# Moving one 1.7 MB load two places down the SyncE queue in the opening of a sparse GATv2 + GCN kernel

## The chip, the cores and the metric

One Trainium2 chip, one core. The metric is the device time of the whole program in microseconds, as a median of runs. A profiled execution is a separate execution of the same program, with its own time.

## What is computed

The input is a feature matrix `x` (3327 x 128, padded to 3328 rows, 26 blocks of 128) and a dense-stored adjacency `adj` (3328 x 3328, float32, about 2% of it nonzero). Two graph layers run one after the other, each on a layer-normed and rectified copy of `x`, and each is added back to `x`:

```
# layer 0: four GATv2 heads
E   = leaky_relu(h @ w1 [:,None,:] + h @ w2 [None,:,:])   # every pair i,j
s   = exp(8 * tanh((E @ a) / 8)) * adj                    # zero where adj is zero
s   = s / sum(s, -1)
out = leaky_relu(s @ h @ Wlin.T)      # heads concatenated, then @ w
# layer 1: GCN
relu(D^-1/2 (adj + I) D^-1/2 @ (h @ W.T + b))
```

Because `adj` zeroes most pairs, the kernel only forms the pairs of each row's nonzero columns. It lists them per row, and gathers the features of those columns.

## The kernel before

**Tables.** In DRAM there are two tables of 3329 rows x 720 floats. One row belongs to one graph node j. Columns 64 and up hold j's features, its part of the score and its products `h_j @ w2` for four heads; columns 0 to 63 hold the adjacency weights of j towards 64 rows of the block in work, so table 0 serves the lower half of a block (`hb` = 0) and table 1 the upper half (`hb` = 1). Columns 64 and up are built once, in the opening, as seven "images" in SBUF (`img`, lines 1022 to 1064, four blocks of 128 nodes each, the last one two blocks) and are stored to both tables by `store(i, t)` (L1041 to L1043; 1312 KB each, 656 KB for the last). Columns 0 to 63 are written anew for each half block by `weights(b, hb)` (L568 to L573), a DRAM to DRAM copy of 832 KB from the transposed adjacency `AT_d`.

**One block.** `load(b)` (L340 to L342) brings the 128 adjacency rows of block b into `adjb`, a pool of one buffer, so a load must wait until the block before it is done with the buffer; the last reader is the row sum at L426. `prep(b)` (L344 to L545) then codes the nonzeros on VectorE (L401), picks them with max instructions (L405 and after), transposes the rows on TensorE (L355), copies them out on ScalarE (L357) and stores them to `AT_d` from ScalarE's queue (L360). The pairs of a half block are processed in nine groups: `gather` (L551 to L566) issues indirect gathers from GpSimd (L562), one for each of eight slots of a buffer `g`; each such window of eight serves two groups, four windows and a smaller one (`ge`, three gathers) make a half block. `stage_z` (L576) transposes a group's rows on TensorE into `z` (L587) and applies the relu as a maximum on VectorE (`r`, L599); `stage_r` (L604) multiplies by `a` (L610); `finish` (L614) does the softmax weights and the weighted sum.

**Order.** Everything is under a hand-written schedule. The main loop (L1146 to L1159) walks over the groups, and `slot()` (L812) between them advances the preparation of the next block by a fixed amount and issues gathers. So each engine's instruction order is fixed when the program is built, and an engine that waits for one instruction holds up all that stands behind it. SyncE (SP) issues `x`, `adj`, the image stores, `weights` and the `hTb` loads, all in one DMA queue (q1 on the page); ScalarE's DMAs are q10, GpSimd's gathers q0.

**The opening.** L1104 to L1135 compute the seven images, store each to table 0 as soon as it is done (L1064), prepare block 0 in between, and then store all seven to table 1 (L1128, L1129). In this last loop, `load(1)` stands behind one of the stores. After it come `weights(0, 1)`, the end of block 0's preparation and the main loop.

**Buffers that overlap.** The four gather buffers (`pg0` to `pg3`, L1138, 23,040 bytes in each partition) are opened when the images' pools (10,496 bytes each, L963) are closed, and lie in the same SBUF. By the addresses of the built program, `pg0` covers the small constants and image 0; `pg1` covers the last 544 bytes of image 0, images 1 and 2 and the first part of image 3; `pg2` covers the rest of image 3, image 4 and the first part of image 5; `pg3` the rest of image 5 and image 6. A gather into `pg1` therefore waits until images 0 to 3 have been stored to table 1, one into `pg2` until images 4 and 5 have, one into `pg3` until image 6 has.

Of the kernel before, what the change touches and what calls it, by code (L numbers as in the profile page):

```python
# [228 lines left out]
def _sparse_layers(tc, nc, x, adj, w1, w2, a, wlin, w, gw, gb, gb_sb, gwT, x_sb, dinv, flag, ident, out):  # L229
# [15 lines left out]
    NB = NP // P  # L245
# [8 lines left out]
    with ExitStack() as l0:  # L254
# [85 lines left out]
        def load(b):  # L340
            blks[b].adjb = pa.tile([P, NP], F32, name="adjb")
            nc.sync.dma_start(blks[b].adjb, adj[b * P:(b + 1) * P, :])  # L342
# [225 lines left out]
        def weights(b, hb):  # L568

            assert blks[b].turned  # L570
            c0 = b % 4 * P + HALF * hb
            nc.sync.dma_start(tables[hb][:NP, :HALF].rearrange("(p r) c -> p r c", p=P),
                              AT_d[b // 4 * NP:(b // 4 + 1) * NP, c0:c0 + HALF].rearrange("(p r) c -> p r c", p=P))  # L573
# [197 lines left out]
        def advance(upto):  # L771

            for b in range(NB):
                while done[b] < NPREP and b * NPREP + done[b] < upto:
                    if next(preps[b], "end") == "end":
                        done[b] = NPREP
                    else:
                        done[b] += 1
                        assert done[b] < NPREP
# [171 lines left out]
        with tc.tile_pool(name="pre", bufs=1) as pre, ExitStack() as images:  # L951
# [36 lines left out]
            def norm(b0, n):  # L988

                st6 = pre.tile([P, n, 6], F32, name=f"st{b0}")  # L990
                for k in range(n):
                    nc.vector.bn_stats(st6[:, k], x_sb[:, b0 + k])
                    nc.vector.bn_aggr(mean[:, b0 + k], st6[:, k])
                var = pre.tile([P, n], F32, name=f"var{b0}")
                nc.vector.tensor_scalar(var, mean[:, b0:b0 + n, 1], EPS, None, op0=OP.add)
                neg = pre.tile([P, n], F32, name=f"neg{b0}")
                nc.vector.tensor_scalar(neg, mean[:, b0:b0 + n, 0], -1.0, None, op0=OP.mult)
                rstd = pre.tile([P, n], F32, name=f"rstd{b0}")
                for _ in inv_root(rstd, var):
                    pass  # L1000
                cen = cens[b0]
                for k in range(n):
                    if b0:
                        nc.gpsimd.tensor_scalar(cen[:, k], x_sb[:, b0 + k], neg[:, k:k + 1], 0.0, op0=OP.add, op1=OP.max)
                    else:
                        nc.scalar.activation(cen[:, k], x_sb[:, b0 + k], AF.Relu, bias=neg[:, k:k + 1], scale=1.0)
                return cen, rstd

            def weights_of_scores():


                nc.vector.tensor_mul(prod, w2_sb, a_bc)
                nc.vector.tensor_reduce(wa[:, :H], prod, AX.X, OP.add)
                nc.vector.tensor_mul(prod, w1_sb, a_bc)
                nc.vector.tensor_reduce(wa[:, H:2 * H], prod, AX.X, OP.add)
                nc.vector.tensor_scalar(wa[:, 2 * H:], wa[:, H:2 * H], SLOPE, None, op0=OP.mult)
                nc.vector.tensor_scalar(wa[:, :H], wa[:, :H], SLOPE, None, op0=OP.mult)

            K = -(-NB // 4)
            imgs, hTs = {}, {}  # L1020

            def features(i):

                b0, n = 4 * i, min(4, NB - 4 * i)
                img = room[i]
                nc.gpsimd.memset(img[:, :n, P + H:PROJ - FEAT], 1.0)
                nc.gpsimd.memset(img[:, :, COLS - FEAT:], 0.0)
                cen, rstd = normed.pop(b0)
                nc.vector.tensor_mul(img[:, :n, :P], cen, rstd[:, :, None].to_broadcast([P, n, D]))
                imgs[i] = img  # L1030

            def turn(i):
                b0, n = 4 * i, min(4, NB - 4 * i)
                pt = ps_s.tile([P, BANK], F32, name="s")
                for k in range(n):
                    nc.tensor.transpose(pt[:, k * P:(k + 1) * P], imgs[i][:, k, :P], ident)
                hTs[i] = turned[i % 2]
                nc.scalar.copy(hTs[i][:, :n * P], pt[:, :n * P])
                nc.scalar.dma_start(hT_d[:, b0 * P:(b0 + n) * P], hTs[i][:, :n * P])

            def store(i, t):  # L1041
                b0, n = 4 * i, min(4, NB - 4 * i)
                nc.sync.dma_start(tables[t][b0 * P:(b0 + n) * P, FEAT:].rearrange("(b p) c -> p b c", p=P), imgs[i][:, :n, :])  # L1043

            def products(i):

                b0, n = 4 * i, min(4, NB - 4 * i)
                img, hT = imgs[i], hTs.pop(i)
                pzs = []
                for k0 in range(0, n, 2):  # L1050
                    pz = ps_z.tile([P, 2, BANK], F32, name="z")
                    for k in range(min(2, n - k0)):
                        nc.tensor.matmul(pz[:, k, :], hT[:, (k0 + k) * P:(k0 + k + 1) * P], w2_sb.rearrange("p h d -> p (h d)"),
                                         start=True, stop=True)
                    pzs.append(pz)
                px = ps_a.tile([P, 2, 256], F32, name="ag")[:, 0, :12 * H].rearrange("p (k c) -> p k c", k=4)
                for k in range(n):
                    nc.tensor.matmul(px[:, k, :], hT[:, k * P:(k + 1) * P], wa, start=True, stop=True)
                for k0, pz in zip(range(0, n, 2), pzs):
                    m = min(2, n - k0)  # L1060
                    nc.scalar.copy(img[:, k0:k0 + m, PROJ - FEAT:COLS - FEAT], pz[:, :m, :])
                nc.scalar.copy(img[:, :n, P:P + H], px[:, :n, :H])
                nc.scalar.copy(p_all[:, b0:b0 + n, :], px[:, :n, H:])
                store(i, 0)  # L1064
# [25 lines left out]
            with tc.manual_schedule():  # L1090
                normed = {}

                def norms():
                    lo, hi = spans.pop(0)
                    cen, rstd = norm(lo, hi - lo)
                    for b0 in range(lo, hi, 4):
                        part = slice(b0 - lo, min(b0 + 4, hi) - lo)
                        normed[b0] = cen[:, part], rstd[:, part]

                def ahead(n):  # L1100
                    while len(made) < min(n, K):
                        made.append(features(len(made)))

                made = []  # L1104
                norms()
                ahead(1)
                advance(2)
                weights(0, 0)
                turn(0)
                blks[0].hTb = pb.tile([P, P], F32, name="hTb")  # L1110
                nc.sync.dma_start(blks[0].hTb, hT_d[:, :P])
                weights_of_scores()
                if len(spans):
                    norms()
                ahead(3)
                products(0)
                if K > 1:
                    turn(1)
                if len(spans):
                    norms()  # L1120
                ahead(5)
                for i in range(1, K):
                    if i + 1 < K:
                        turn(i + 1)
                    products(i)
                    advance(2 + NCODE * i / (K - 1))
                    ahead(i + 3)
                for i in range(K):  # L1128
                    store(i, 1)  # L1129
                    if i == min(1, K - 1) and NB > 1:  # L1130
                        load(1)
                weights(0, 1)
                advance(NLIST)
                turn_parameters()
                advance(NPREP)  # L1135
# [93 lines left out]
def kernel(  # L1229
# [26 lines left out]
    gb_sb = const.tile([P, D], F32, name="gb_sb")  # L1256

    _sparse_layers(tc, nc, x, adj, w1, w2, a, wlin, w, gw, gb, gb_sb, gwT, x_sb, dinv, flag, ident, out)


# [46 lines left out]
```

## Time and profile before

| | us |
|---|---|
| median of three runs | 3246.03 (3227.53, 3246.03, 3260.07) |
| profiled execution, its own time | 2536.74 |
| span of the profiled execution | 2534.9 |
| TensorE busy | 2278.9 (90%) |
| VectorE busy | 2030.5 (80%) |
| GpSimd busy | 1791.8 (71%) |
| mean granted TensorE clock | 0.980 |

DMA moved 838.58 MB at a mean of 331 GB/s, and its busy share is 9 tenths or more in all but the last of the 40 slices. The span is counted from the first to the last instruction of the program; the profiled execution is 709 us shorter than the median of the runs, and the page does not say where the runs spend these 709 us.

How to read the views: in the timeline a row is "start, duration, engine, line, operation, out<-in, count", and what stands in square brackets is how long the engine sat idle before it and what ended that. An entry of SPq is the issuing of a DMA, not its data. In the queue view a row gives a DMA queue's packets, its MB and the time that they took as a share of 16 DMA engines in that stretch. In the view by stretches a row gives each engine's busy time and, at the end, the granted TensorE clock, the DMA busy share and GB/s.

### The profile page before, as it was taken

Reading aid. Unit: us, or ns where it says so; the run is one execution under the profiler, and the core shown is the slowest. Engines: PE = TensorE matmul, PEld = TensorE weight load, DVE = VectorE, ACT = ScalarE, POOL = GpSimd, SP = SyncE. Lnnn points to the kernel's source line nnn. Section 1 sums busy time; section 2 is a strip of 40 time slices with the busy share of each in tenths; the row PEclk is TensorE's granted clock in tenths of the full one; section 3 lists DMA queues with packets and bytes.
Section 4 is the critical chain, followed back from the end, with each engine's and each line's share of the span. In section 5 each row is a group of like instructions: output and inputs, shape, how many; then the busy total and the mean of one; then the engine's idle time right before and its main releaser. Section 6 shows DMA issues by size and latency. Waiting matters only on the chain.

```text
span 2534.9 us, 51974 instructions
## 1 busy us (share of the span) xinstructions
PE 2278.9 (90%) x19410; PEld 1586.2 (63%) x19410; DVE 2030.5 (80%) x6260; ACT 704.1 (28%) x1651; POOL 1791.8 (71%) x1873
## 2 busy tenths in 40 slices
PE   6689899988989998989998999999999899999898
PEld 4456666656666666666666666666666667675553
DVE  7678988888788888878888788988988888895433
ACT  4122233223223222322322322232232233222110
POOL 3577777777777777777777777777777777777620
PEclk9789999999999999999999999999999999999999
DMA  9999999999999999999999999999999999999995
GB/s 294 392 338 314 342 353 318 334 351 335 324 339 346 318 328 359 329 319 343 337 312 336 353 311 341 352 329 329 339 346 318 330 360 313 333 322 347 324 336 186
DMA packets 460759, 838.58 MB, mean 331 GB/s; under 512 B 209099, under 2 KB 318165, under 8 KB 457173
## 3 DMA queue, kind: packets, MB, share of 16 engines
q0 software_dynamic: 145600, 640.34, 71.0%
q1 hardware_dynamic: 219396, 140.96, 19.1%
q10 hardware_dynamic: 95504, 53.88, 7.0%
q8 instruction: 156, 2.56, 0.4%
q14 instruction: 103, 0.84, 0.1%
HBM read 765.93 MB, written 113.42 MB: 347 GB/s over the span
## 4 chain that ended last, share of the span: by engine, by line
PE 35%; DVE 24%; DMA 20%; POOL 11%; issue 7%; ACT 1%; SPq 0%; DVEq 0%; POOLq 0%; ACTq 0%
DMA g<-table,idx 13%; DVE r L599 11%; POOL g L562 10%; PE z L587 10%; PE s L610 6%; PE z L590 3%; DMA ge<-table,idxo 3%; PE z L937 2%; DVE cand L405 2%; PE tr L627 2%; PE ag L658 2%; DMA AT_d<-at 2%; PE tr L370 2%; PE tr L505 1%; DVE codes L401 1%
## 5 line engine op out<-in xcount | busy, mean ns | idle before, releaser
L562 POOL DMA_INDIRECT g<-table,idx x1664 | 1616.3, 971 | 568.3 <-issue 442.2
L599 DVE TENSOR_TENSOR r<-z,x1n 128x1024 f32<-128x1024 f32 x832 | 1010.1, 1215 | 65.5 <-PE z L587 63.9
L587 PE MATMUL z<-ident,g 128*128 128x128 f32 x6656 | 922.4, 278 | 151.9 <-DVE r L599 111.7
L587 PEld LDWEIGHTS z<-ident,g 128*128 128x128 f32 x6656 | 743.8, 142 | 366.9 <-DVE r L599 224.2
L610 PE MATMUL s<-r,sel 128*32 128x512 f32 (+1 forms) x3744 | 491.1, 597 | 0.7 <-ACT ssb L618 0.7
L618 ACT COPY ssb<-s 128x512 f32<-128x512 f32 x260 | 146.7, 564 | 524.6 <-PE s L610 522.5
L630 DVE TENSOR_TENSOR sc<-tr,g 128x32 f32<-128x32 f32 x208 | 38.5, 185 | 300.5 <-PE tr L627 300.5
L405 DVE MAX8 cand<-codes 128x8 f32<-128x52 uint16 x1664 | 215.3, 205 | 0.0
L562 POOL DMA_INDIRECT ge<-table,idxo x156 | 152.6, 978 | 47.5 <-issue 38.1
L638 ACT ACTIVATE th<-sc 128x32 f32<-128x32 f32 x260 | 58.3, 224 | 420.9 <-DVE sc L633 418.5
L590 PE MATMUL z<-oi,x1b 128*128 128x384 f32 x416 | 174.1, 501 | 0.0
L658 PEld LDWEIGHTS ag<-g,wt 128*32 128x32 f32 x3328 | 99.0, 110 | 115.3 <-issue 100.8
L357 ACT COPY at<-tr 128x512 f32<-128x512 f32 (+1 forms) x175 | 97.0, 554 | 222.2 <-PE tr L355 198.3
L627 PE MATMUL tr<-ident,ssb 128*128 128x128 f32 x988 | 153.1, 276 | 5.0 <-ACT ssb L618 4.5
L610 PEld LDWEIGHTS s<-r,sel 128*32 128x32 f32 x3744 | 73.9, 108 | 110.5 <-issue 86.4
L587 PEld LDWEIGHTS z<-ident,ge 128*128 128x128 f32 x624 | 81.4, 146 | 94.8 <-issue 28.5
L596 ACT ACTIVATE r<-z 128x768 f32<-128x768 f32 x104 | 84.3, 810 | 201.7 <-PE z L590 201.7
L658 PE MATMUL ag<-g,wt 128*32 128x133 f32 x3328 | 133.4, 278 | 0.0
L587 PE MATMUL z<-ident,ge 128*128 128x128 f32 x624 | 111.7, 283 | 21.1 <-DMA ge<-table,idxo 18.5
L627 PEld LDWEIGHTS tr<-ident,ssb 128*128 128x128 f32 x988 | 114.3, 141 | 15.3 <-ACT ssb L618 14.9
L355 PE MATMUL tr<-ident,adjb 128*128 128x128 f32 x676 | 107.4, 282 | 16.3 <-DMA adjb<-in_adj_dram 10.2
L401 DVE SCALAR_TENSOR_TENSOR codes<-adjb,code 128x832 uint16<-128x832 f32 x104 | 102.3, 1020 | 1.9 <-DMA adjb<-in_adj_dram 1.9
(188 smaller groups left out, 2350.4 us busy)
## 6 DMA issues: line engine op xcount, KB each, us to landing
adjb<-in_adj_dram SPq DMA_DIRECT2D x26, 1664.0 KB
table<-AT_d SPq DMA_DIRECT2D x52, 832.0 KB
AT_d<-at ACTq DMA_DIRECT2D x150, 256.0 KB
g<-table,idx POOLq DMA_INDIRECT x1664
table<-img SPq DMA_DIRECT2D x12, 1312.0 KB
adjb<-AT_d SPq DMA_DIRECT2D x18, 512.0 KB
g<-AT_d SPq DMA_DIRECT2D x7, 1024.0 KB
g<-AT_d ACTq DMA_DIRECT2D x5, 1024.0 KB
```

Of the source, the lines that this page charges most:

```text
L355: nc.tensor.transpose(pt[:, q, :], adjb[:, (j0 + q) * P:(j0 + q + 1) * P], ident)
L357: nc.scalar.copy(at[:, :n, :], pt[:, :n, :])
L401: nc.vector.scalar_tensor_tensor(codes[:, i], adjb[:, c0:c0 + part], 0.0, code[:, c0:c0 + part], op0=OP.not_equal, op1=OP.mult, accum_out= ...
L405: nc.vector.max(cand[:, c, 8:].rearrange("p (r s) -> p r s", s=32)[:, :, sgm % 32], codes.rearrange("p a b -> p (a b)")[:, sgm % 32 * SEG: ...
L562: return nc.gpsimd.indirect_dma_start(out=g[:, t, lo:COLS], out_offset=None, in_=tab, in_offset=bass.IndirectOffsetOnAxis(ap=at[:, t:t + 1 ...
L587: nc.tensor.matmul(z[:, i, q * P:(q + 1) * P], g[:, m % 2 * 4 + q, PROJ + h * D:PROJ + (h + 1) * D], ident, is_transpose=True, start=(q == ...
L590: nc.tensor.matmul(z[:, i, :n], k.x1b[:, h * D:(h + 1) * D], k.oi[:, hb * n:(hb + 1) * n], start=False, stop=True, skip_group_check=True)
L599: nc.vector.tensor_tensor(r.rearrange("p h (i s) -> p h i s", s=16), z.rearrange("p h (i s) -> p h i s", s=16), k.x1n[:, 2 * hp:2 * hp + 2 ...
L610: nc.tensor.matmul(k.s[32 * h:32 * h + 32, :n], sel[:, h, 31 - at:63 - at], rs[h // 2][:, h % 2, :n], start=(at == 0), stop=(at == 1 or m ...
L618: nc.scalar.copy(ssb[:, :nk * P], s[:, :nk * P])
L627: nc.tensor.transpose(pt[:, q, :], ssb[:, q * P:(q + 1) * P], ident)
L658: nc.tensor.matmul(ag[32 * cg:32 * cg + 32, u, :WORK], wt[:, t].rearrange("p h q -> p (h q)"), g[:, t, FEAT:FEAT + WORK], start=(w == 0 an ...
```

## The change

```diff
@@ -1127,7 +1127,7 @@
                     ahead(i + 3)
                 for i in range(K):
                     store(i, 1)
-                    if i == min(1, K - 1) and NB > 1:
+                    if i == min(3, K - 1) and NB > 1:
                         load(1)
                 weights(0, 1)
                 advance(NLIST)
```

K is 7. In the built program no engine but SP has another order. On SP's queue the load of block 1's adjacency rows (1664 KB), which stood between the table 1 stores of images 1 and 2, now stands between those of images 3 and 4:

```
 L1043 DMACopy table_74<-img_160 128x4x656
 L1043 DMACopy table_74<-img_164 128x4x656
-L342 DMACopy adjb<-in_adj_dram 128x3328
 L1043 DMACopy table_74<-img_168 128x4x656
 L1043 DMACopy table_74<-img_172 128x4x656
+L342 DMACopy adjb<-in_adj_dram 128x3328
 L1043 DMACopy table_74<-img_176 128x4x656
 L1043 DMACopy table_74<-img_180 128x4x656
```

No instruction is added or removed. Which stores a gather waits for stays the same; only the semaphores that carry these waits are dealt out anew.

## The prediction

> **What bounds the kernel now.** I read the page first, then the view by stretches, then the chain of waits in order of time, the timelines of SP, GpSimd, VectorE and TensorE from 55 to 140 us, and the queue view by stretches. The stretches show two regimes (columns: span; busy time and count of PE, PEld, DVE, ACT, POOL; clock; DMA share; GB/s):
>
> ```profile
> 90.00:99.00 9.00, 0.00 (x0) 0.00 (x0) 2.74 (x10) 0.58 (x1) 6.72 (x7) 0.70 1.06 396
> 99.00:133.00 34.00, 27.12 (x210) 18.00 (x211) 25.99 (x84) 7.49 (x14) 25.23 (x27) 0.88 1.05 397
> 190.00:1200.00 1010.00, 913.96 (x8168) 644.10 (x8168) 856.47 (x2633) 293.99 (x698) 762.86 (x785) 0.99 0.99 335
> ```
>
> From 190 us on TensorE is busy 90% of the time and DMA runs at 335 GB/s. In the opening DMA moves 396 GB/s and TensorE stands still for 9 us. So the steady part is bound by compute, and the change can act only in the opening, where the bytes are the bound. The chain of waits agrees: its longest piece is the table 1 stores.
>
> ```profile
> 61.27 0.87 SPq L342
> 62.18 1.24 SPq L1043
> 63.47 26.13 DMA table<-img
> 89.75 0.70 issue
> 90.45 4.21 DMA g<-table,idx
> 94.97 7.64 DMA g<-table,idx
> 102.65 2.18 PE z L587 x9
> ```
>
> GpSimd issues the first window (w0) at 67.13 to 77.6 us, and then waits for image 3's store before the second (w1); TensorE waits for w1's rows:
>
> ```profile
> 90.45 1.71 POOL L562 DMA_INDIRECT g<-table,idx  x1 [12.88 <-DMA table<-img]
> ...
> 99.19 0.45 PE L587 MATMUL z<-ident,g 128*128 128x128 f32 x1 [9.97 <-DMA table<-img]
> ```
>
> The second row starts 99.19 - 90.45 = 8.7 us after the gather was issued; its release is put down to a store, but what it reads is the gather. On VectorE, block 1's coding of the adjacency stands in front of the first relu:
>
> ```profile
> 73.63 0.22 DVE L536 TENSOR_TENSOR pmx<-tmask,p_all 128x64 f32<-128x64 f32 x1
> 75.73 1.03 DVE L401 SCALAR_TENSOR_TENSOR codes<-adjb,code 128x832 uint16<-128x832 f32 x1 [1.88 <-DMA adjb<-in_adj_dram]
> ...
> 81.34 1.23 DVE L599 TENSOR_TENSOR r<-z,x1n 128x1024 f32<-128x1024 f32 x1 [3.63 <-PE z L587]
> ```
>
> The load is already awaited for 1.88 us, but the relu then waits 3.63 us for TensorE: the load may come 3.63 us later at no cost.
>
> **What the Trainium skill says.** "DMA: Bandwidth & Descriptors", section "Queues, rings and completion order": one queue's descriptors are consumed in ring order on each DMA engine, and an engine with work in several queues goes round between them a packet at a time. The trace agrees. From 76 to 84 us gathers and stores run together, one packet against one (gather packets are twice as long):
>
> ```profile
> q0 software_dynamic: 482, 2.10, 64.0%
> q1 hardware_dynamic: 481, 1.22, 38.3%
> ```
>
> So moving the load changes who is served first in q1, and not how many bytes must pass. The same page, section "Anatomy of one DMA", puts about 2 us of a transfer's fixed cost on the receipt of its last write; here image 3's store waits about 3 us between data and release (worked out below). "TensorE: Matmul & The Clock Gate", Part 1, says that the clock is halved after about 3.4 us without work; here it is 0.70 in the idle stretch above, so a moved idle stretch moves a slow clock too.
>
> **The change part by part.** Nothing is added or removed. The load moves behind two stores, and the stores of images 2 and 3 move ahead of 1.70 MB. Neither semaphore waits nor their holders on other engines change.
>
> *The two stores.* In q1 the load's data begin about 69.2 us and end about 74.1: 1.70 MB at some 350 to 400 GB/s. Image 2's data will begin at 69.2 instead. A store is 1.34 MB in 512 packets. Alone, q1 moves about 380 GB/s, 145 packets each us, until the gathers of w0 arrive at 72.3: 3.1 x 145 = 450. The remaining 574 of 1024 share the engines at 481 / 8 = 60 each us: 9.6 us, to 82.0 us. Before, image 3's data ended at about 87.4 us (535 packets by 84.0, then about 143 each us), and the gather followed at 90.45, 3.0 us later. So w1's first gather goes at about 85.0, **5.5 us earlier**, and its first row reaches TensorE at 85.0 + 8.7 = 93.7.
>
> *The load.* It begins at 82.0 and takes 1.70 MB / 0.39 = 4.4 us, to 86.5. Before, VectorE started 1.7 us after the data's end (75.73 - 74.1), so L401 starts at 88.2, **12.5 us later**. Less 3.6 us of slack, the first relu is 8.9 us late, at 90.2. Behind L401 on VectorE stand w0's four relus and 32 maxima; on TensorE, behind the transposes of `adjb` (82.73 us before), the rest of w0. Behind these wait ScalarE's copies L357 and the `AT_d` stores, which all come some 6 to 9 us later. SP is not held: nothing on it needs block 1's rows until the load of block 2 at 119.76 us.
>
> *Where the two meet.* From the first relu to the last code of block 1 VectorE worked from 81.34 to 92.78 us with 0.4 us idle, so it needs 11.1: from 90.2 it is through at 101.3. Then it can do w1's first relu, which came at 104.02 before because its rows came at the gathers' pace. Rows for it are there at 102.65 - 5.5 = 97.1, so it comes at 101.3: **2.7 us earlier**. TensorE's idle stretch of about 10 us before w1 goes to the time of the late load instead.
>
> *What is late next.* The third window, w2, needs images 4 and 5 stored. Ahead of these in q1 are the same bytes as before; but w1's gathers now start to move at about 85.0 + 5.5 = 90.5 (first packets came 5.5 us after the issue before) and share with them. From 86.5 to 90.5 about 140 packets each us pass: 560 of 1024; the other 464 at 55 each us (the `AT_d` stores share too) take 8.4 us, to 98.9. With 3.0 us to the release w2's gathers start at 101.9; before, they started at 101.20, straight behind w1's at 1.25 us each. So w2, w3 and `ge` come 0.7 us **later**, and the 5.5 us won at w1 are given back there. From w2 on the order is as before: `ge`'s rows let TensorE go on at 132.74, just in time, and the gathers into table 1's first window waited at 125.80 us for `weights(0, 1)`, which also stands behind all seven stores. DMA runs at 397 GB/s until 133 us in this kernel, so what is served early there is paid by something else before 133: the sum of bytes is the same.
>
> *The sum.* -2.7 us at w1's first relu, which nobody downstream can use; +0.7 at w2, and 0 to 2 us for `weights(0, 1)` and a TensorE clock that is slow at another time. I take +1 us on the span: 2534.9 + 1 = 2535.9, and 2536.74 + 1 = 2537.7 for that execution. The runs are 3246.03 / 2536.74 = 1.28 times as long, and the profile doesn't say why; if all their waits are longer in that ratio, +1 is +1.3: **3247 us**.
>
> Bounds: if w2 needn't wait for its stores, the gain is between 2.7 us (VectorE) and 5.5 us (gathers). If VectorE's stall isn't made up, the loss is 8.9 us, and 12.5 at most if the slack is used otherwise. Below and above these I see no reason, for bytes and instructions are the same.
>
> **The rivals.** *Gathers win.* Images 4 and 5 land by 96 us, and all windows come earlier: -2.7 to -5.5 us, times 1.28 -3.5 to -7: about 3241. For it: GpSimd issues without a break from 90.45 on, so its chain of 1.25 us gathers sets when `ge` comes. Against: the two stores have no fewer bytes in front of them.
>
> *The late load costs.* This is the one on the slower side: `adjb` is late on VectorE and TensorE, whose order is fixed. It decides when L401 starts later than 88.2 + 2.7 = 90.9 us; from there each us is one us at the end. The price at 12.5 to 16 us of delay is small, but if the idle stretch also shifts block 1's `AT_d` stores into w2's rows and thereby the load of block 2, the whole 8.9 to 12.5 us remain: times 1.28 +11 to +16, about 3260. For it: 93.73 us already has ScalarE waiting 5.91 us for an `AT_d` store. Against: TensorE was idle at 89 to 99 us in any case.
>
> *The change does nothing*: excluded, the load is moved in the built queue and its buffer is free (L426 ended at 61.1 us).
>
> **How the numbers follow.** Near nothing (span within 3 us) 0.50; gathers win 0.20; the late load costs 0.22; something in the runs that the profiled execution doesn't show 0.08. All three mechanisms stay below 0.5%. A difference of 1%, about what a measurement of this kernel can tell from no change, is 32 us, and the three runs lie 32.5 us apart; it can come from that scatter or from the last case alone, which I weigh a little to the slower side since the stall acts on two engines: faster by over 1% 0.13, within 1% 0.70, slower by over 1% 0.17. The likeliest case alone with the runs' scatter gives 3228 to 3266. With the rivals and the unexplained 709 us the range is 3200 to 3300.
>
> **What would show it.** In the profile after: L401 of block 1 at about 88 us with some 14 us waited for the load; w1's first gather at about 85 and w2's at about 102; w1's first relu at 101 to 102; `ge`'s group on TensorE within 2 us of 132.7; from 190 us on no difference. The prediction is wrong if that group comes over 4 us earlier or later, or if the steady stretch differs.

## The result and the profile after

| | before | after |
|---|---|---|
| median of 22 runs each, us | 3235.97 (3219.59 to 3260.07) | 3229.98 (3217.45 to 3239.52) |
| ratio, 95% interval | | 0.9977 [0.996, 0.9995] |
| profiled execution, span | 2534.9 | 3232.6 |
| TensorE busy; mean granted clock | 2278.9; 0.980 | 2569.0; 0.917 |

The change was measured 6 us, or 0.23%, faster: far under the 1% that the prediction takes as what can be told from no change. But its 95% interval leaves out 1, and the forecast was +1 us. The forecast of 3247 us was built on three runs of before with a median of 3246.03; 22 runs have 3235.97, so 10 of the 17 us between 3247 and 3229.98 lie in that base. One thing must be known to read the profiles: this program has two paces, about 2530 and about 3230 us, whatever the order in the queue; all runs of one comparison share a pace, but the profile of before was taken at the first and that of after at the second. So the two may be compared in the opening, where the paces differ little up to some 100 us, and not in the steady part.

The page of the kernel after shows the pace: its row for the gathers (columns after the bars: busy us, mean ns; idle us before them, and what ended most of it, with its us) says that GpSimd now waits 590 us for buffers which TensorE has yet to read.

```profile
span 3232.6 us, 51975 instructions
...
PE 2569.0 (79%) x19410; PEld 1759.7 (54%) x19410; DVE 2052.9 (64%) x6260; ACT 689.3 (21%) x1651; POOL 1799.9 (56%) x1873
...
L562 POOL DMA_INDIRECT g<-table,idx x1664 | 1627.7, 978 | 1142.2 <-PE ag L658 590.0
```

The same three stretches of the kernel after as the prediction showed of before:

```profile
90.00:99.00 9.00, 7.38 (x43) 6.02 (x43) 7.17 (x30) 1.17 (x2) 1.30 (x2) 0.63 1.03 412
99.00:133.00 34.00, 17.10 (x98) 10.12 (x97) 13.97 (x56) 6.62 (x10) 18.90 (x20) 0.72 1.04 370
190.00:1200.00 1010.00, 803.09 (x6340) 550.92 (x6333) 674.92 (x2052) 225.63 (x545) 604.29 (x617) 0.93 0.84 262
```

TensorE, which stood still from 90 to 99 us, is busy for 7.4 of these 9 us. From 99 to 133 us it does 17 us of work where it did 27, but here the paces already differ: the change at the pace of before does 21.8 (e1_after_again, below). The timelines of GpSimd and VectorE in the kernel after:

```profile
80.71 0.94 POOL L562 DMA_INDIRECT g<-table,idx  x1 [2.24 <-DMA table<-img]
...
104.39 0.94 POOL L562 DMA_INDIRECT g<-table,idx  x1 [11.52 <-ACT at L357]
```

```profile
86.01 1.02 DVE L401 SCALAR_TENSOR_TENSOR codes<-adjb,code 128x832 uint16<-128x832 f32 x1 [12.15 <-DMA adjb<-in_adj_dram]
...
87.91 1.22 DVE L599 TENSOR_TENSOR r<-z,x1n 128x1024 f32<-128x1024 f32 x1
```

The first gather of w1 goes 9.7 us earlier than the 90.45 of before, L401 starts 10.3 us later than 75.73 and the first relu stands directly behind it. The first gather of w2 is 3.2 us later than 101.20. It is put down to ScalarE's copy L357, but by the built program it waits for the stores of images 4 and 5, whose last packets (2624 bytes each in q1) pass at 101.9 us. In the kernel before it waited for no store; it stood in the unbroken row behind w1:

```profile
101.20 0.95 POOL L562 DMA_INDIRECT g<-table,idx  x1 [0.30 <-issue]
```

The queue view from 76 to 84 us still has one packet against one, although the load's larger packets are now among them:

```profile
q1 hardware_dynamic: 301, 2.05, 63.7%
q0 software_dynamic: 297, 1.30, 40.7%
```

The chain of waits has another longest piece. In the kernel after it goes through w0's gathers and a store of the transposed adjacency, which ScalarE awaits:

```profile
72.53 11.98 DMA g<-table,idx
84.55 3.04 PE z L587 x13
...
93.69 12.39 DMA AT_d<-at
106.16 0.59 ACT at L357
```

At the 2530 pace (the kernel after again, the first experiment below) it goes through the table 1 stores as before, only further, 35.04 us long instead of 26.13, to the store that w2 waits for, and from there without a break of note on GpSimd:

```profile
66.97 35.04 DMA table<-img
...
102.08 0.70 issue
102.78 7.47 DMA g<-table,idx
```

### The profile page after: what moved, and what is told of

The parts are those of the page before. It is cut to its first block, busy times and chain, and to the rows that moved or that the text cites. A ratio compares the mean times of both kernels' runs of the same rounds, so it can differ in the third digit from the quotient of the medians.

```text
span 3232.6 us, 51975 instructions
## 1 busy us (share of the span) xinstructions
PE 2569.0 (79%) x19410; PEld 1759.7 (54%) x19410; DVE 2052.9 (64%) x6260; ACT 689.3 (21%) x1651; POOL 1799.9 (56%) x1873
## 4 chain that ended last, share of the span: by engine, by line
PE 52%; DVE 17%; another core or an unknown queue 11%; issue 9%; ACT 6%; DMA 4%; POOL 1%; ACTq 0%; DVEq 0%; SPq 0%; POOLq 0%
PE z L587 18%; PE s L610 9%; DVE r L599 8%; PE tr L627 4%; PE z L590 4%; DMA g<-table,idx 3%; PE ag L676 2%; ACT r L596 2%; PE ag L658 2%; PE tr L355 2%; PE tr L370 2%; DVE cand L405 2%; PE z L937 2%; ACT ssb L618 1%
## 5 line engine op out<-in xcount | busy, mean ns | idle before, releaser
L599 DVE TENSOR_TENSOR r<-z,x1n 128x1024 f32<-128x1024 f32 x832 | 1012.3, 1218 | 411.9 <-remote 239.1
L587 PE MATMUL z<-ident,g 128*128 128x128 f32 x6656 | 1027.8, 299 | 296.8 <-DVE r L599 135.8
L587 PEld LDWEIGHTS z<-ident,g 128*128 128x128 f32 x6656 | 838.2, 154 | 535.4 <-DVE r L599 231.6
L610 PE MATMUL s<-r,sel 128*32 128x512 f32 (+1 forms) x3744 | 537.6, 609 | 12.5 <-issue 10.5
L658 PE MATMUL ag<-g,wt 128*32 128x133 f32 x3328 | 202.4, 280 | 99.2 <-issue 98.4
L627 PE MATMUL tr<-ident,ssb 128*128 128x128 f32 x988 | 178.4, 307 | 106.0 <-ACT ssb L618 77.0
L658 PEld LDWEIGHTS ag<-g,wt 128*32 128x32 f32 x3328 | 123.2, 110 | 248.7 <-issue 239.4
L357 ACT COPY at<-tr 128x512 f32<-128x512 f32 (+1 forms) x175 | 97.3, 556 | 345.3 <-remote 133.0
L610 PEld LDWEIGHTS s<-r,sel 128*32 128x32 f32 x3744 | 83.0, 110 | 158.0 <-issue 144.3
L370 PE MATMUL tr<-at,x_sb 128*128 128x128 f32 x488 | 80.2, 309 | 91.5 <-ACT at L357 64.1
L370 PEld LDWEIGHTS tr<-at,x_sb 128*128 128x128 f32 x488 | 66.6, 209 | 115.7 <-ACT at L357 83.0
```

The lines of the kernel that those rows point to most:

```text
L370: nc.tensor.matmul(pq[:, :P], x_sb[:, j0 + q, :], at[:, q, :], start=(q == 0), stop=(q == js[-1]))
L587: nc.tensor.matmul(z[:, i, q * P:(q + 1) * P], g[:, m % 2 * 4 + q, PROJ + h * D:PROJ + (h + 1) * D], ident, is_transpose=True, start=(q == ...
L599: nc.vector.tensor_tensor(r.rearrange("p h (i s) -> p h i s", s=16), z.rearrange("p h (i s) -> p h i s", s=16), k.x1n[:, 2 * hp:2 * hp + 2 ...
L610: nc.tensor.matmul(k.s[32 * h:32 * h + 32, :n], sel[:, h, 31 - at:63 - at], rs[h // 2][:, h % 2, :n], start=(at == 0), stop=(at == 1 or m ...
L627: nc.tensor.transpose(pt[:, q, :], ssb[:, q * P:(q + 1) * P], ident)
L658: nc.tensor.matmul(ag[32 * cg:32 * cg + 32, u, :WORK], wt[:, t].rearrange("p h q -> p (h q)"), g[:, t, FEAT:FEAT + WORK], start=(w == 0 an ...
```

## The experiments

Each was measured beside the unaltered kernel before, and the ratio is to that. The labels with the same number were measured together. The columns after the ratio are times within the run's own profile, in us: L401 of block 1, the first relu (L599), the first gather of w1, w1's first relu, the first gather of w2, and the first gather from table 1 (the upper half of block 0).

| run | median, us | ratio [95%] | L401 | relu | w1 | w1 relu | w2 | upper |
|---|---|---|---|---|---|---|---|---|
| e1_before_again | 2531.5 | 0.9998 [0.9988, 1.0007] | 74.4 | 80.0 | 89.3 | 102.6 | 99.8 | 124.7 |
| e1_after_again | 2534.34 | 1.0004 [0.9991, 1.0016] | 86.0 | 87.9 | 81.2 | 98.8 | 102.8 | 127.6 |
| e1_behind_third | 2532.25 | 0.9996 [0.9987, 1.0004] | 78.9 | 83.4 | 89.3 | 103.0 | 100.0 | 124.8 |
| e1_behind_sixth | 2542.83 | 1.0032 [1.0018, 1.0046] | 101.5 | 103.4 | 80.7 | 114.4 | 98.5 | 134.8 |
| e2_after | 2537.94 | 1.0013 [0.9999, 1.0026] | 88.5 | 90.5 | 83.5 | 101.3 | 104.8 | 129.3 |
| e2_image3_last | 2535.44 | 1.0007 [0.9995, 1.0018] | 86.2 | 88.1 | 91.2 | 105.1 | 101.2 | 125.0 |
| e3_prepare_later | 2534.8 | 1.0007 [0.9995, 1.0018] | 94.5 | 81.7 | 82.9 | 96.6 | 103.6 | 128.0 |
| e3_prepare_later_alone | 2534.23 | 1.0006 [0.9997, 1.0016] | 88.1 | 80.7 | 89.7 | 103.7 | 100.0 | 124.1 |
| e4_pe_paced_before | 2973.91 | 1.1749 | 75.3 | 82.7 | 89.8 | 105.0 | 100.5 | 125.7 |
| e4_pe_paced_after | 2978.0 | 1.1765 | 88.0 | 89.9 | 82.7 | 102.7 | 103.8 | 128.5 |
| e5_after | 2536.76 | 1.002 [1.0008, 1.0031] | 88.9 | 90.8 | 84.1 | 101.8 | 105.2 | 129.8 |
| e5_before | 2533.42 | 1.0011 [0.9999, 1.0023] | 76.3 | 81.9 | 91.0 | 104.7 | 101.8 | 126.3 |
| e6_three_before | 2994.62 | 1.1815 | 75.2 | 80.8 | 89.5 | 102.7 | 100.5 | 132.4 |
| e6_three_after | 2993.76 | 1.1808 | 87.7 | 89.6 | 82.6 | 100.5 | 103.8 | 133.0 |
| e7_after | 3235.89 | 1.0008 [0.9989, 1.0026] | 87.0 | 88.9 | 81.9 | 99.8 | 103.0 | 130.7 |
| e7_before | 3231.93 | 0.9998 [0.9973, 1.0023] | 75.7 | 81.5 | 90.3 | 104.1 | 101.1 | 138.8 |

**Where the load stands** (e1). The same two kernels again, and the load one place earlier and two places later than in the change:

```diff
-                    if i == min(1, K - 1) and NB > 1:
+                    if i == min(2, K - 1) and NB > 1:   # behind_third
+                    if i == min(5, K - 1) and NB > 1:   # behind_sixth
                         load(1)
```

> The kernel before, unchanged, to have a profile of it beside those of the other runs, on one chip. Time: a ratio of 1.000 within 0.002. Both theories expect the same of it. From its profile, if it is about 3230 us long as the runs are: block 1's L401 near 76 us, the first window's relu near 81 us, the second window's gathers (w1) near 90 us, its first relu near 104 us, and blocks of about 119 us from there.

> The changed kernel, unchanged. Theory G (w1's gathers come earlier, and what they win in the opening is kept to the end): ratio 0.998, and the whole difference of 5 to 10 us to the kernel before stands in the profile at the end of block 0, with blocks of the same length from there. Rival S (the difference isn't made in the opening; the steady blocks come out a little shorter or the two are equal and the 0.2% was chance): ratio 0.998 or 1.000, and at the end of block 0 the two profiles are within 2 us of each other.

> The load stands behind image 2's store, one place later than before and one earlier than in the change; w1's buffer needs image 3's store too, which is behind the load again. Theory G: w1's gathers start near 90 us as before, and the time is that of before, ratio 1.000. If it were the load's own lateness or its distance from the first two stores that helps (rival), half of the gain would come: 0.999.

> The load stands behind image 5's store: images 4 and 5, which w2's buffer needs, are stored ahead of it too. Theory G: w2's gathers come right behind w1's (no wait of 11.5 us as in the change), worth up to 5 us more: ratio 0.996 to 0.998. Rival L (the late load costs): block 1's rows come near 96 to 100 us instead of 86, VectorE's first relu waits for them, and 8 to 12 us are lost against the change: ratio 1.000 to 1.002.

All four ran at the 2530 pace. There the change gains nothing: +0.04%, with the kernel before at -0.02% beside itself. Behind the third store, w1 stays at 89.3 us, so it is image 3's store that w1 needs. Behind the sixth, w2 starts before the load has landed, and then the load is what everything waits for (timelines of GpSimd and of VectorE):

```profile
98.46 0.95 POOL L562 DMA_INDIRECT g<-table,idx  x1 [8.07 <-DMA table<-img]
134.79 0.94 POOL L562 DMA_INDIRECT g<-table,idx  x1 [12.21 <-DVE cand L436]
```

```profile
101.48 1.02 DVE L401 SCALAR_TENSOR_TENSOR codes<-adjb,code 128x832 uint16<-128x832 f32 x1 [27.62 <-DMA adjb<-in_adj_dram]
```

L401 is 27.0 us later than in e1_before_again. The upper half's first gather, which waits for VectorE's `cand`, comes 10.0 us later, and the median is 10.3 us over the kernel before in the same comparison (2532.56). This is the prediction's second rival, and its rule fits: one us lost for each us of L401 after 90.9 us makes 10.6 us. It is one point. In the change itself L401 stays at 86 to 89 us.

At the same pace, the stretches of e1_after_again show the steady part unchanged (before: 913.96 of TensorE, 762.86 of GpSimd, 335 GB/s):

```profile
99.00:133.00 34.00, 21.83 (x142) 14.81 (x142) 22.40 (x75) 7.08 (x12) 22.11 (x24) 0.79 1.07 378
190.00:1200.00 1010.00, 915.63 (x8172) 644.24 (x8171) 858.00 (x2634) 293.98 (x698) 762.41 (x784) 0.99 0.99 334
```

The gain at w1 and the loss at w2 come out of one view, q1 and the gathers' queue q0 in e1_after_again from 85 to 97 us, and in the kernel before from 85 to 94 us:

```profile
q0 software_dynamic: 670, 2.89, 61.5%
q1 hardware_dynamic: 672, 1.72, 36.1%
```

```profile
q1 hardware_dynamic: 1243, 3.18, 90.8%
q10 hardware_dynamic: 721, 0.36, 13.4%
```

In the kernel before, no gather's packets ran in this stretch, and q1 passed 138 packets each us. With w1's gathers there early it passes 56, one for one with q0. This agrees with the Trainium skill, "DMA: Bandwidth & Descriptors", section "Queues, rings and completion order": an engine goes round the queues that have work, a packet at a time. So images 4 and 5 land later: their last packets pass at 100.5 us in e1_after_again and at 94.3 in e1_before_again. Of these 6.2 us, w2 sees 3.0, since before it stood behind w1's gathers and not behind its stores.

**Taking the early w1 away** (e2). The load stays behind the fourth store, but image 3 is stored behind it, so that w1 cannot start early:

```diff
-                for i in range(K):
+                for k, i in enumerate((0, 1, 2, 4, 3, 5, 6)):
                     store(i, 1)
-                    if i == min(1, K - 1) and NB > 1:
+                    if k == 3:
                         load(1)
```

> The changed kernel once more, to see which of two results it repeats. Theory C (the 0.2% gained belongs to a chip on which the steady blocks are slow, about 119 us each and 3230 us in all; where the blocks take 88 us and the whole 2530 us, the change is worth nothing): ratio 0.997 to 0.999 if the kernel before takes about 3230 us here, 1.000 to 1.001 if it takes about 2530. Rival (chance in the first comparison): 1.000 on either.

> The change with the table 1 stores of images 3 and 4 exchanged: the load is as late as in the change (L401 near 86 us), but w1's buffer is released behind it, near 90 us as in the kernel before, so the early w1 gathers are taken away and the late load stays. Theory W (w2's stores are the next gate, so an early w1 is worth nothing): the time of the change within 0.001. Rival G (the early w1 makes up for the late load): slower than the change by the 4 us that its first relu was earlier, 0.0015 or more.

> The kernel before, for a profile on this chip. About 3230 us or about 2530 us long, nothing between.

w1 falls back to 91.2, w2 goes back to 101.2 and the upper half's first gather to 125.0. VectorE's stall of 12.9 us for the load remains, and the time hardly moves: 2535.44 against 2537.94 us of the change, with intervals that overlap. A gain of the early w1 of 4 us and more (rival G) would have made this run slower than the change; it is not. The run shows where w2's delay comes from: without w1's early gathers, w2 waits for no store (0.30 us before it, as in the kernel before). But it takes away the early w1 and the late w2 together, so it does not price the two apart. A single execution of the kernel before has 101.2 and 126.2 us for the two gathers (2531.49 us).

**Taking VectorE's stall away** (e3). Block 1's preparation is held back by about twelve slots, with the load where the change puts it, and alone:

```diff
-            advance(NPREP * (1 + t + min(1.0, t) * AHEAD))
+            advance(NPREP * (1 + (t + min(1.0, t) * AHEAD if t > 2 / 3 else max(0.0, 1.8 * t - 0.2))))
```

> The change, and block 1's preparation begins 12 slots later (behind the first window's two groups) and then runs faster, to be where it was at two thirds of the block. The load is as late as in the change (near 86 us), but nothing stands waiting for it. If the late load's stall of the first window is what costs (theory L): the first relu back near 81 us, and the time that of the kernel before or less, 0.998 to 1.000. If the stores are the gate for w2 and the upper half (theory W): w2's gathers near 103 us and the upper half's near 127 us as in the change, ratio 1.0005 to 1.002 where the kernel takes 2530 us.

> The same later preparation with the load at its place in the kernel before: the control for the run with both. Its rows are there in time, so only the crowding of the preparation into the rest of the block can show: ratio 0.999 to 1.002. The difference of the two runs is the load's place alone, without a stall: theory W +0.001 for the later load, theory L 0 or less.

The first relu is back at 81.7 us and w1's first relu comes as early as 96.6, 7.1 us earlier than in the control. Nothing of this arrives: w2 is still at 103.6, the upper half at 128.0, and both ratios are the same, 1.0007 and 1.0006. So neither the stall nor the early relu has a price that these runs could show. The control, with w2 3.6 us earlier, comes out no faster either: with intervals of some 3 us to either side, 3 us can't be seen. What w2's delay costs is read from the next pair.

**TensorE as the bound** (e4). To get below the scatter and to put another engine at its limit, the transposes of most groups are done twice, the second result over the first; the output is the same:

```diff
-                    for q in range(n // P):
+                    for q in list(range(n // P)) * (2 if m < 8 else 1):
                         nc.tensor.matmul(z[:, i, q * P:(q + 1) * P], ...
```

> The kernel before with TensorE made the pace: each transpose of the gathered rows at L587 (not those of the overflow group) is done twice, the second over the first, 6656 more of about 0.14 to 0.28 us: some 900 us more on TensorE, 3250 to 3500 us in all, and GpSimd waiting for buffers instead of issuing without a break. The reference for the next run.

> The change with the same doubled transposes. Theory P (the change gains only where TensorE sets the pace, for then TensorE's early start on w1 is kept and the later w2 gathers are still in time): shorter than the run before this one by 3 to 7 us (0.001 to 0.002), and w1's and all later groups of block 0 come 3 to 7 us earlier in its profile. Rival W everywhere (the opening's bytes are the gate whoever sets the pace): equal or 1 to 4 us longer.

TensorE is then busy in 1008.87 of 1010 us in both kernels (the row of the kernel with the change):

```profile
190.00:1200.00 1010.00, 1008.87 (x9331) 808.10 (x9333) 740.20 (x2217) 247.52 (x593) 660.39 (x672) 1.00 0.90 286
```

This is the cleanest pair. The upper half's first gather is 2.8 us later, its first relu 2.2 us later (146.1 against 143.9), the last gather of the whole kernel 2.2 us later (2858.2 against 2856.0), the span 2.6 us longer, and the medians differ by 4.1 us (2972.99 to 2976.17 against 2976.92 to 2979.23, no overlap). Of the 3.3 us lost at w2, 2.1 to 2.2 stand at the start of every block that was read (blocks 1 to 5, 8, 12, 16, 20, 24 and 25) and at the last gather.

**Once more with a control** (e5): the change and the kernel before, unaltered.

> The changed kernel once more, as a further draw. Where the kernel before takes about 3230 us: ratio 0.997 to 0.9995 if the first comparison's gain belongs to that pace, 1.000 if it was particular to that comparison. Where it takes about 2530 us: 1.0004 to 1.0013 as twice before, by 2 to 3 us that the gathers of block 0's upper half come later.

> The kernel before beside it, for a profile at the same pace. If it takes about 3230 us, its blocks are about 119 us long as in the changed kernel's first profile, and the difference of the two stands either at the end of block 0 (opening) or grows from block to block (steady part). If about 2530 us: ratio 1.000, and nothing new.

The ratio is 1.002 [1.0008, 1.0031] for the change, and 1.0011 [0.9999, 1.0023] for the kernel before beside itself. A difference of 0.1% is what identical kernels show here, so the change's three values at this pace (+0.04, +0.13, +0.20%, mean +0.12% or 3 us) say "0 to 5 us slower" and no more.

**Three gather buffers instead of four** (e6), to make GpSimd wait for TensorE's reading as it does at the 3230 pace:

```diff
-            return pgs[state["turn"] % 4].tile([P, WT, ROW], F32, name="g")
+            return pgs[state["turn"] % 3].tile([P, WT, ROW], F32, name="g")
-        state = {"slot": 0, "fetched": 0, "g": 4, "ge": 1}
+        state = {"slot": 0, "fetched": 0, "g": 3, "ge": 1}
-        pgs = [... for i in range(4)]
+        pgs = [... for i in range(3)]
```

> The kernel before with three gather buffers instead of four: GpSimd must wait for TensorE to free a buffer in every window, as in the 3230 us profile (590 us waited there), and no engine is busy all the time. 2700 to 3300 us. The fourth window's gathers wait for the first buffer instead of for images 5 and 6. The reference for the next run.

> The change with three gather buffers. Theory B (where the round of buffers sets the pace, and neither the gather stream nor a full TensorE, the change gains, as in the first comparison): 5 to 8 us shorter than the run before this one (0.002). Rival W (the opening's order costs 2 to 4 us whatever sets the pace): 0 to 8 us longer, since the first window's buffer is freed later by the late load's stall and the fourth window waits for it.

GpSimd then waits as it does at the 3230 pace (e6_three_before):

```profile
POOL g L562 <- PE ag L658: 511.1, 163, 11.0
```

The change makes no difference that six runs each could show: 2993.76 against 2994.62, with runs from 2972 to 3000. w2 is 3.3 us later, but the upper half only 0.6 us: w3 and the upper half wait for TensorE to read a buffer in both kernels, and each wait is 1.4 us shorter with the change (4.2 for 5.6, then 1.5 for 2.9).

**At the pace of the recorded result** (e7), the same two kernels:

> The changed kernel as a further draw. If the kernel before takes about 3230 us here: 0.997 to 0.9995 if the first gain belongs to that pace; 1.000 within 0.002 if that pace only lets the opening's 2 to 3 us drown, as with three buffers. If it takes about 2530 us: 1.0004 to 1.002 again.

> The kernel before beside it: a ratio of 1.000 within 0.0015, and a profile at the same pace as the changed kernel's.

The gain did not come back: 1.0008 [0.9989, 1.0026]. All runs at this pace together, 44 of the change and 69 of before, have means of 3233.5 and 3234.6 us: a difference of -1.1 us, with 3.4 us to either side at 95%. The spans of the two profiles are 3243.0 and 3243.1.

The openings differ more at this pace. In the profile of e7_before ScalarE stood still for 22 us and TensorE behind it (waits of ScalarE, then the stretch 100 to 140 us; columns of a wait: us in total, times, longest):

```profile
ACT ssb L618 <- remote: 153.7, 23, 22.2
```

```profile
100.00:140.00 40.00, 17.84 (x114) 12.35 (x115) 13.74 (x53) 6.04 (x9) 19.69 (x21) 0.65 0.84 298
```

With the change TensorE did 23.07 us of work in that stretch (e7_after). A stall of this kind is in all three profiles at this pace: ScalarE's wait is 16.6 us in e7_after and 16.4 in the first profile of after, and it ends at 130.0, 131.4 and, in e7_before, 128.6 us. With the change eight relus were done before the stall, in e7_before six; the next came at 129.8, 131.2 and, in e7_before, 131.7 us. So the upper half's first gather came 8.1 us earlier (130.7 against 138.8), its first relu 7.0 us (158.5 against 165.5) and block 1's first gather 4.7 us (192.1 against 196.8). But this lead is over one profile of before, and it is gone later: at three quarters of the way (the 641st of 832 relus) the change stands at 2447.7 and 2427.7 us in its two profiles, before at 2446.0.

## Why the prediction was right and wrong, step by step

**The two stores, w1 earlier: right, under-sized.** 85.0 was forecast; 80.7 to 84.1 was measured in seven profiles. Two terms were too long. The last packets of image 3 were forecast at 82.0 and passed at 79.6 in e1_after_again, and its release took 1.6 us there and not 3.0.

**The load, L401 and the first relu: right, partly by luck.** 88.2 and 90.2 were forecast; 86.0 to 88.9 and 87.9 to 90.8 were measured. The stall on VectorE is 12.2 to 14.4 us long in the seven profiles; 14 was forecast. Two errors made up for each other: in e1_after_again the load's packets begin at 79.0 and not at 82.0, but w0's gathers still share the engines, and it takes 6.0 us and not 4.4.

**w1's first relu: right.** 2.7 us earlier was forecast; 2.2 to 4.4 was measured in the pairs of one comparison and one pace. VectorE's work from the first relu to this one, forecast as 11.1 us, takes 11.0 in e1_after_again.

**w2 later: right in sign, mis-sized.** +0.7 us was forecast; +3.0 (e1), +3.3 (e4) and +3.5 (e5) were measured, and +1.9 at the 3230 pace (e7). The term that failed is "From 86.5 to 90.5 about 140 packets each us pass: 560 of 1024". It took from the kernel before that w1's first packets come 5.5 us after the issue. In the change w1's gathers stand directly behind w0's in a queue that is not empty between 73 and 99 us (e1_after_again), so the stores get 56 packets each us from the beginning: 672 in 12 us. The 1024 packets took 16.1 us, from 84.4 to 100.5, where 12.4 was forecast. (A gather's packets are 1.7 times as long as a store's by the lines shown from 76 to 84 us, not twice; no sum uses it.)

**"From w2 on the order is as before": wrong.** The prediction named a sign: the last group of the half block (`ge`'s) on TensorE within 2 us of its old time, and wrong beyond 4. It comes 7.1 us later in e1 and 5.6 in e5 (137.7 against 132.1), but 2.2 in e4 (138.1 against 135.9). The first row is e1_before_again, the second e1_after_again:

```profile
130.95 0.79 PE L587 MATMUL z<-ident,ge 128*128 128x128 f32 x3
138.05 0.55 PE L587 MATMUL z<-ident,ge 128*128 128x128 f32 x3
```

Another load has moved. In e1 SyncE issues the load of block 2 at 113.39 us and not at 118.17. Its packets pass from 116.0 to 123.5 us and not from 121.6 to 128.8, and now meet the first of w3's gathers, for which TensorE waits. That this is the cause is read from the times; no run holds that load back. At the 2530 pace most of this delay on TensorE is made up again: block 1's first gather is 2.4 us later in e1 and 3.3 in e5.

**"The sum of bytes is the same", so nearly nothing: right.** The early gathers took their turn from the stores, and the next window paid for it. Neither the early w1 nor the stall shows in the time: e2 takes away the first (and the late w2 with it), e3 the second, and the time stays within the intervals.

**"So the steady part is bound by compute": wrong for that profile.** At the 2530 pace TensorE is busy 90% of the time, but GpSimd issues almost without a pause. Its waits in e1_before_again:

```profile
POOL g L562 <- issue: 447.5, 1455, 1.9
```

1455 of the 1820 gathers follow the one before after 0.31 us on average, with nothing to wait for. A block has 70 gathers, each 0.95 us and a gap of 0.30: 87.5 us, and from gather 700 to gather 1400 of this profile a block takes 90.1 us (978.8 to 1880.2 us for ten). So by the profile what counts at this pace is when the unbroken row of gathers gets to the upper half's first gather (no run makes a gather cheaper, to prove it), and that is 2.9 us later in e1, 2.8 in e4, 3.5 in e5. The forecast of +1 us was of the same kind, with 0.7 for w2 where 3.0 was measured. The weaker rule that the opening's end counts did hold: in e4, where TensorE is the bound, 2.2 us arrive.

**"If all their waits are longer in that ratio, +1 is +1.3": wrong.** For the recorded number this is the step that failed: it carries a sum worked at the 2530 pace over to runs at the 3230 pace, with its sign. The 709 us are not longer waits of the same kind. At the 3230 pace GpSimd waits for TensorE:

```profile
POOL g L562 <- PE ag L658: 576.6, 173, 14.3
...
PEld ag L658 <- issue: 226.0, 498, 2.0
```

(e7_before; in e1_before_again the second row is 99.6 us, 330 times, at most 0.8). So in the opening w2's stores are not what ends last there. The upper half's first gather waits for TensorE, a wait that the sum put at nothing: 14.3 us in e7_before and 3.5 in e7_after, so that it comes 8.1 us earlier although w2 is 1.9 us late. Whether this made the 6 us of the first comparison is open, for the gain did not come back in e7. No engine is busy all the time then, a block takes 118 us, and TensorE stands still before weight loads that wait for no semaphore: from 190 us on 259 to 281 times for over 0.4 us, 184 to 202 us in all, in three profiles at this pace, and 65 to 75 times, 36 to 41 us, in three at the other. An example from e7_after, 1.4 us from one product to the next, which have all they need:

```profile
124.15 0.42 PE L658 MATMUL ag<-g,wt 128*32 128x133 f32 x1 [1.02 <-issue]
125.55 0.38 PE L658 MATMUL ag<-g,wt 128*32 128x133 f32 x1 [0.98 <-issue]
126.93 0.38 PE L658 MATMUL ag<-g,wt 128*32 128x133 f32 x1 [1.01 <-issue]
```

What holds TensorE there is not settled; the difference of these idle times is some 155 of the 709 us, and whether the rest follows from them was not tried.

**The rivals.** "Gathers win" is refuted as it was put, with images 4 and 5 early and all windows with them: w2 comes later in every pair. "The late load costs" is real but begins further out (e1_behind_sixth). The recorded -6 us is of the size that "gathers win" gave, but not shown to be its doing: w2 was 3.2 us late in that very profile, and the repeat gave +0.08%. So the cause of the -6 us stays open, chance included. What also stays open is whether the shorter stall between 105 and 130 us at the 3230 pace (6 to 7 us at the upper half's first relu, two profiles of the change against one of before) is a property of the order; the pooled runs leave room for a gain of 4 us and for a loss of 2. Several profiles of each kernel at that pace would tell.

## What to carry to other kernels

A transfer moved within one full queue changed, here, little more than who waits: follow the bytes to the next consumer, expect the window that got ahead to take its packets from the one behind it, and look at what else the queue's owner issues sooner. Before calling a stretch bound by the busiest engine, look for the engine that never waits, even if its busy share is only 70%. And when profile and runs stand 28% apart, trust no difference of a few tenths of a per cent before it has come twice, and no sum that was worked at the other pace: compare a kernel with itself first.

## What was unexpected of the hardware

The same program runs at about 2530 or about 3230 us, with a mean TensorE clock of 0.98 or 0.917, and nothing in the program chooses. One indirect gather costs 1.25 us on GpSimd at both (0.95 and a gap of 0.30). Identical kernels in one comparison differed by 0.02 to 0.11% in the ratio.
